# Filler products in TensorE's planned gaps, and score maxima taken four heads at a time, in a four-layer convolution and attention kernel

## The chip, the cores and the metric

The kernel runs on one core of a Trainium2 chip. The metric is device microseconds of one execution, from the first instruction to the last with what lies around them; lower is better. Seven executions before the change took 10873.29 to 10902.44 us, with a median of 10892.89 us.

Five engines work side by side, each through its own list of instructions in order: TensorE (PE, with its weight loads shown apart as PEld), VectorE (DVE), ScalarE (ACT), GpSimd (POOL) and SyncE (SP), which issues the transfers. TensorE writes its products to PSUM, which has eight banks of 128 x 512 fp32 here, and the others read them from there.

## What is computed

Four layers follow one another on x of shape (8, 256, 32, 32), eight samples of 256 channels and 1024 positions:

```python
# layer 0: attention with 4 heads (key 32, value 64), a 3x3 depthwise term, then a gated feed-forward and 8x8 FFTs
attn = softmax(einsum('bhkn,bhkm->bhnm', q, k) * SCALE)
out = einsum('bhdm,bhnm->bhdn', v, attn)
...
x = gelu(x1) * x2
...
# layer 1: group norm, attention with 8 heads of 32, a small MLP
attn = softmax(einsum('bhdi,bhdj->bhij', q, k) * temp)
...
# layer 2: quantised 1x1, 3x3, 1x1 convolutions, with integer codes
# layer 3: a Mamba block over four directions of the image (selective scan with 16 states)
x = _L0_conv_ref(x, ...); x = _L1_conv_ref(x, ...); x = _L2_conv_ref(x, ...); x = _L3_conv_ref(x, ...)
```

Softmax needs, for each of the 1024 rows of each head, the maximum over 1024 scores and the sum of exponentials. The change touches layers 0 to 2 only.

## The kernel before

**Two phases.** `phase_a` (line 258) does layers 0, 1 and 2 for all eight samples, `phase_b` (line 1059) layer 3. Each has a planner of its own. Nothing of `phase_b` is changed.

**The planner.** Work is written as Python generators ("strands") that yield one operation, or a list of operations on one engine with a cost, or a condition to wait for. `_Order.run` (line 231) keeps a planned clock for each engine. Again and again it takes, of all strands that are not waiting for a condition, the one whose operation could start first by the plan (ties by rank), emits it, and moves the engine's planned end (`free[e]`, line 253). The planned start is `_Order.start` (line 218): the latest of the engine's planned end, the planned ends of what the operation reads and overwrites, and 0.35 us (`LATENCY`) more where another engine did that. The order of instructions on each engine is thereby fixed when the program is built, and the scheduler of the framework adds the waits on the chip but moves nothing (`manual_schedule`, line 1041). All instructions are emitted by one helper, so the profile puts all of them on line 132 and groups are told apart by their tiles.

**Rooms.** A `_Room` (line 152) is a set of equal buffers. `left` lists those not taken, in the order in which they were put back; `take` takes the first. A buffer is put back when the plan *emits* its last reader, with the planned end of that reader, plus 0.35 us, kept in `last[tag, k]`; the next tile in that buffer has this as its `base`, before which nothing may write it. `bank` (line 287) is the room of the eight PSUM banks.

**Who uses banks.** The strand of a sample (`sample`, line 1020; layers at 653, 754, 865 and 956) takes single banks by `side()` for its projections. `maxima` (line 513) computes, for each head, each 128 rows (`t`) and each half of the keys (`j`), one bank of scores; VectorE takes the negated maximum of each row, ScalarE the exponentials with their sum. `MAXIMA` = 2 strands `some()` (line 520) share the list `todo` of (t, j, h) with h = 0 or 2, and take two heads at a time. Each head's product has 32 rows of the array (keys of 32 channels), and head h + e uses rows 32(h + e) to 32(h + e) + 31. `exponentials` (line 574) makes the attention itself: one bank for the output and, in each step, four banks of scores (cost `SCORES` = 1.3: four products of 32 rows, then four of 3 rows that subtract the maxima by means of the bf16 constant `minus`, -1.0 in 128 x 128, line 313), four exponentials on ScalarE, and four value products (`values`). Only one call of `exponentials` runs at a time: it fills `attending` while it runs. There are three calls of 16 steps for each sample, 24 in all.

**The limit on lent banks.** `may(n)` (line 395) is true when n banks are left and, while a call of `exponentials` is running, no more than `OTHERS` = 3 banks are then lent to everything else. So a set of four can't be lent while a call runs.

## Time and profile before

| | |
|---|---|
| median of 7 executions | 10892.89 us |
| the profiled execution | 10899.64 us |
| its span, first to last instruction | 10897.8 us |
| mean granted TensorE clock | 0.927 |
| TensorE busy | 9825.0 us (90%) |
| VectorE busy | 8475.8 us (78%) |
| ScalarE busy | 8686.1 us (80%) |
| GpSimd busy | 6713.9 us (62%) |
| maxima on VectorE (TENSOR_REDUCE of stats) | 1536, 979.9 us |
| last attention step of `phase_a` ends at | 3741 us |

The span runs from 0 to 10897.8 us on the profile's clock. `phase_a` fills about the first third; the numbers of the 40 slices show the seam as a jump in GpSimd's share and in the transferred bytes after the fourteenth slice. "Granted clock" is the share of TensorE's full clock that the hardware let through; in this execution it is always either 0.5 or 1. A busy share of TensorE counts a slowed product with its whole, longer duration. A product of fp32 operands shows as two matrix multiplications in the profile, one of bf16 operands as one.

### The profile page before, as it was taken

What the parts mean: (1) busy time and instruction counts of PE and PEld (TensorE: products, weight loads), DVE (VectorE), ACT (ScalarE), POOL (GpSimd) and SP (SyncE); (2) the same over time, 40 slices, a digit from 0 to 9 for tenths busy, and PEclk for the clock granted to TensorE, in tenths of its full rate; (3) what the DMA queues carried; (4) which work ended last, traced back from release to release, by engine and by line L of the source; (5) the groups of instructions that cost most, each with busy time, mean ns of one, the idle gap of its engine ahead of it and who ended that gap; (6) DMA issues with size and microseconds to landing.
All of it is one profiled execution on the core that took longest, in us unless ns stands there. A gap on an engine that the chain in (4) does not pass through costs nothing. (4 is left out here: it accounts for less than half of the span.)

```text
span 10897.8 us, 154085 instructions
## 1 busy us (share of the span) xinstructions
PE 9825.0 (90%) x56992; PEld 6320.2 (58%) x57104; DVE 8475.8 (78%) x9005; ACT 8686.1 (80%) x16270; POOL 6713.9 (62%) x3732
## 2 busy tenths in 40 slices
PE   8788998989999889999999999999989999999998
PEld 3233433333333257777777777777777777777776
DVE  4666556664735559898988998999889899898897
ACT  7666776777767568888989888888888888888887
POOL 2323012122221158888888888888888888888887
PEclk7778988888798789999999999999999999999999
DMA  1000000000000011111111111111111111111111
GB/s 38 5 4 5 2 9 6 8 2 9 5 3 1 12 38 48 47 47 52 50 41 56 44 46 54 45 48 53 45 49 48 50 48 46 51 50 42 55 42 46
DMA packets 210549, 367.85 MB, mean 34 GB/s; under 512 B 24241, under 2 KB 68657, under 8 KB 208770
## 3 DMA queue, kind: packets, MB, share of 16 engines
q1 hardware_dynamic: 209794, 358.00, 11.2%
q8 instruction: 448, 7.34, 0.3%
q14 instruction: 307, 2.51, 0.1%
HBM read 333.26 MB, written 14.16 MB: 32 GB/s over the span
## 5 line engine op out<-in xcount | busy, mean ns | idle before, releaser
L132 POOL TENSOR_TENSOR h<-h,cb 128x1024 f32<-128x1024 f32 x2048 | 4876.7, 2396 | 903.0 <-ACT st L132 440.5
L132 ACT ACTIVATE da<-dt,am 128x512 f32<-128x512 f32 x4096 | 2870.2, 713 | 512.4 <-DVE h L132 504.0
L132 DVE TENSOR_TENSOR_SCAN h<-da,st,db 128x512 f32<-128x512 f32 x2048 | 2468.6, 1259 | 177.4 <-PE db L132 96.1
L132 DVE TENSOR_TENSOR_SCAN h<-da,db 128x512 f32<-128x512 f32 x2048 | 2345.4, 1198 | 236.9 <-PE db L132 155.2
L132 ACT ACTIVATE dbu<-du,bT 128x512 f32<-128x512 f32 x3584 | 2474.9, 709 | 36.3 <-PE db L132 34.0
L132 PE MATMUL db<-ident,dbu 128*128 128x128 f32 x14336 | 2218.7, 280 | 177.2 <-DVE h L132 148.3
L132 PE MATMUL py<-ident,h 128*128 128x128 f32 x16384 | 2122.8, 275 | 91.9 <-POOL h L132 84.6
L132 PEld LDWEIGHTS db<-ident,dbu 128*128 128x128 f32 x14336 | 1671.4, 143 | 709.2 <-DVE h L132 375.2
L132 PEld LDWEIGHTS py<-ident,h 128*128 128x128 f32 x16384 | 1843.5, 141 | 169.0 <-POOL h L132 138.1
L132 DVE TENSOR_REDUCE stats<-bank 128x1 f32<-128x512 f32 x1536 | 979.9, 682 | 612.5 <-PE bank L132 610.7
L132 ACT ACTIVATE bank<-bank,stats 128x512 f32<-128x512 f32 x1536 | 1032.6, 691 | 393.8 <-DVE stats L132 387.9
L132 PE MATMUL bank<-big,big 32*128 32x512 f32 x4096 | 1075.7, 748 | 51.7 <-ACT bank L132 34.1
L132 POOL TENSOR_TENSOR mid<-mid,mid 128x961 f32<-128x961 f32 (+2 forms) x192 | 400.8, 2095 | 1064.6 <-ACT mid L132 700.8
L132 ACT ACTIVATE exps<-bank 128x512 f32<-128x512 f32 x1536 | 796.7, 619 | 259.2 <-PE bank L132 258.6
L132 PE MATMUL pp<-xi,cvd 128*128 128x512 f32 x2048 | 947.6, 606 | 9.6 <-ACT xs L132 3.4
L132 PE MATMUL db<-dg,du 128*128 128x128 f32 x4096 | 811.0, 280 | 0.0
L132 PEld LDWEIGHTS bank<-big,big 32*128 32x128 f32 x4096 | 427.7, 213 | 590.7 <-ACT bank L132 272.5
L132 POOL TENSOR_TENSOR dt<-dt,tmp 128x512 f32<-128x512 f32 x512 | 653.2, 1276 | 168.6 <-DVE tmp L132 146.5
L132 DVE TENSOR_TENSOR tmp<-dt,xs 128x512 f32<-128x512 f32 x256 | 603.4, 2357 | 191.9 <-POOL dt L132 191.7
L132 PEld LDWEIGHTS db<-dg,du 128*128 128x128 f32 x4096 | 638.0, 197 | 0.0
L132 PEld LDWEIGHTS pp<-xi,cvd 128*128 128x128 f32 x2048 | 378.1, 195 | 402.9 <-issue 387.9
L132 PE MATMUL bank<-big 32*128 32x512 f32 x2048 | 527.9, 740 | 53.0 <-ACT bank L132 43.5
(184 smaller groups left out, 11062.8 us busy)
## 6 DMA issues: line engine op xcount, KB each, us to landing
cb<-c_d SPq DMA_DIRECT2D x1024, 256.0 KB, 3.2
wi<-w_in SPq DMA_DIRECT2D x192, 192.0 KB, 3.5
cdb<-codes SPq DMA_DIRECT2D x48, 256.0 KB, 4.1
big<-in_x_dram SPq DMA_DIRECT2D x8, 1024.0 KB, 5.3
big<-big SPq DMA_DIRECT2D x16, 512.0 KB, 6.3
out_dram<-z SPq DMA_DIRECT2D x32, 256.0 KB, 2.5
low<-low SPq DMA_DIRECT2D x16, 128.0 KB, 2.4
codes<-cd SPq DMA_DIRECT2D x16, 128.0 KB, 1.7
```

What stands on the lines that cost most here:

```text
L132: return getattr(getattr(nc, self.engine), self.method)(*self.args, **self.kw)
```

## The change

Three things are added. First, the planner may be given a function `fill`, which it calls before it emits an operation on TensorE, with the planned start. Second, `phase_a` gives it one: it works out how long TensorE has been idle by the plan, counted from the time at which some bank (or the operation's own bank, where that is about to be overwritten) is free by the plan, and emits one product of the constant `minus` with itself (128 x 128 weights, 512 columns, bf16) for each 0.3 us (`FILL`) of it, into that bank, whose content nobody reads. Where it is a bank from the room, the one longest free by the plan is taken, and goes to the end of the list of `left`. The planner's clock isn't moved by these products. Third, `some()` in `maxima` waits until two banks may be lent, and then takes four heads at once where four may be lent and the next entry is h = 0 (it then takes the entry for h = 2 off the list too), two heads otherwise; the four products are one operation with a cost of 1.0 against 0.9.

```diff
@@ class _Order, __init__ and run
+        self.fill = None
...
             t, s = min(((self.start(s[2][1]), s) for s in ready), key=lambda x: (x[0], x[1][0]))
             cost, ops = s[2]
             e = ops[0].engine
+            if self.fill and e == "tensor":
+                self.fill(t, ops)
@@ phase_a, maxima
+    FILL = 0.3
...
             while todo:
+                yield lambda: not todo or may(2)
+                if not todo:
+                    break
+                n = 4 if may(4) and not todo[0][2] else 2
                 t, j, h = todo.pop(0)
-                bb = yield from two()
+                if n == 4 and todo:
+                    todo.pop(0)
+                bb = yield from some_banks(n)
                 ops = []
-                for e in range(2):
+                for e in range(n):
...
-                yield (0.9, ops)
-                for e in range(2):
+                yield (0.9 if n == 2 else 1.0, ops)
+                for e in range(n):
@@ phase_a, before the samples
+    def fill(gap, ops):
+        free, o = order.free.get("tensor", 0.0), ops[0]
+        spare = min(bank.left, key=lambda k: order.last.get((bank.tag, k), 0.0), default=None)
+        own = o.method == "matmul" and o.kw["start"] and o.args[0].shape[-1] == HALF and o.kw["rhs"].shape[0] > 3
+        since = min(
+            [order.last.get((bank.tag, k), 0.0) for k in bank.left] + [order.base.get(o.args[0].name, 0.0)] * own,
+            default=1e9,
+        )
+        n = int((gap - max(free, since)) / FILL)
+        if n < 1:
+            return
+        if spare is not None and order.last.get((bank.tag, spare), 0.0) <= since:
+            bank.left.remove(spare)
+            bank.left.insert(0, spare)
+            t = bank.take()
+        else:
+            t = None
+        out = o.args[0] if t is None else t
+        rhs = minus.unsqueeze(1).to_broadcast([P, 4, P])
+        for _ in range(n):
+            nc.tensor.matmul(out, lhsT=minus[:, : out.shape[0]], rhs=rhs, start=True, stop=True)
+        if t is not None:
+            bank.put(t)
+
+    order.fill = fill
```

## The prediction

> **What bounds the kernel now.** The profile's slices come first: they show where TensorE's clock is held down.

> ```profile
> PE   8788998989999889999999999999989999999998
> PEclk7778988888798789999999999999999999999999
> POOL 2323012122221158888888888888888888888887
> ```

> From the fifteenth slice on (layer 3) the clock is full nine tenths or more; the change doesn't touch that part. In layers 0 to 2 it is 0.7 to 0.9 although TensorE is busy 8 or 9 tenths. The table of stretches over 0 to 3741 us gives a mean of 0.84; as the clock is always 0.5 or 1, 32% of that time is at half clock.

> Next I split layers 0 to 2 by the 24 calls of `exponentials`, each from its first to its last exponential (64 apiece). The calls hold 1584 us, what lies between them 1916, the time before the first 199. Same view, columns as in the first line:

> ```profile
> core 0: us, PE busy (x) PEld busy (x) DVE busy (x) ACT busy (x) POOL busy (x), PEclk, DMA share, GB/s
> 3465.00:3529.00 64.00, 64.00 (x374) 19.93 (x374) 12.20 (x25) 46.16 (x98) 3.03 (x4) 1.00 0.00 1
> 2734.00:2977.00 243.00, 225.52 (x584) 92.38 (x583) 194.65 (x294) 177.75 (x434) 56.80 (x30) 0.77 0.02 6
> 3587.00:3666.00 79.00, 76.60 (x220) 28.90 (x218) 49.17 (x93) 46.65 (x128) 0.00 (x0) 0.50 0.00 1
> ```

> The first is a call: TensorE busy throughout at full clock, nothing else near it. Over the 24 calls TensorE is busy 1556 of 1584 us, clock 0.94. The second lies between calls: clock 0.77, with TensorE, VectorE and ScalarE all loaded. Over all stretches between calls the sums are TensorE 1612, VectorE 1531 and ScalarE 1291 of 1916 us, clock 0.76, so half clock for 2 x (1 - 0.76) = 48% of them. Counting the starts of the maxima's reductions, about 1300 of 1536 fall there or before the first call: calls and maxima take turns.

> What others wait for between calls, from the waits of that second stretch:

> ```profile
> DVE stats L132 <- PE bank L132: 31.1, 18, 4.1
> ```

> The same count over all stretches between calls: 377 us of VectorE's idle time end with a bank from TensorE, and no other cause passes 20. So the calls are bound by TensorE's work, and the rest is a chain in which TensorE, at half clock half of the time, is what VectorE waits for.

> **Why the clock falls.** The third row above is the key: 79 us with TensorE 97% busy, and half clock throughout. The products in it:

> ```profile
> 1518.58 1.93 PE L132 MATMUL bank<-big,w_m 128*64 128x512 f32 x4
> 1520.44 1.13 PE L132 MATMUL bank<-big,big 32*128 32x512 f32 x4
> 1521.50 1.93 PE L132 MATMUL bank<-big,w_m 128*64 128x512 f32 x4
> ...
> 3621.62 1.06 PE L132 MATMUL bank<-mid,codes_w 128*64 128x512 bf16 x2
> 3622.61 3.55 PE L132 MATMUL bank<-big,big 32*128 32x512 f32 x8
> ...
> 3712.64 1.14 PE L132 MATMUL bank<-big,big 32*128 32x512 f32 x8
> 3713.61 0.40 PE L132 MATMUL bank<-low,minus 3*128 3x512 bf16 x4
> 3713.93 1.07 PE L132 MATMUL bank<-exps,big 128*32 128x512 f32 x8
> 3714.93 1.14 PE L132 MATMUL bank<-big,big 32*128 32x512 f32 x8
> ```

> At full clock four passes of 128 rows take 1.86 us start to start, so one takes about 0.43 with the change of shape around it; a pair of heads (four passes of 32 rows) takes 1.06, eight passes of four heads 0.97. So 32-row products of different rows run together, and a pair fills half of the array. At half clock two pairs take 3.55 us. I cut the first 3.8 ms into windows of 3.41 us (all clock stretches but the last are multiples of it) and gave each window its array activity: streaming time of each product (0.427 us for 512 columns of an fp32 pass at full clock, half for bf16, double at half clock) times its share of rows and of columns, over the window. Of 70 half-clock windows with an activity of 0.75 or more, 64 are followed by full clock, of 300 below it 8. Of 54 full-clock windows below 0.3 all are followed by half clock, of 32 from 0.3 to 0.4 18, of 648 above it one. Between, the clock stays as it is. Pairs alone at half clock give about 0.45 (the most crowded bin: 60 windows, two left it). Hence the trap: once slow, a stage of pairs stays slow, however busy.

> [...]

> **The filler products.** One is 128 x 128, bf16, 512 columns: products of that form in layer 3 start 0.216 us apart at full clock (median of 705), 0.427 at half. They fill the whole array: in a window at half clock one adds 0.125 to the activity, so two or three lift a mixed window at 0.45 to 0.75, where it has idle time. At full clock 0.35 of a window is enough to stay up.

> Gain between calls: VectorE's 377 us of waiting for banks is the upper bound. A second way gives the same size: 48% of 1916 us is 914 us at half clock, TensorE about 0.79 busy there, and half of those 720 us, 360, is what half clock costs. The lower bound is nothing: VectorE is already busy 80% there, and its own operations may fill what is freed. I take half: **-190**. Gain in calls: clock 0.94 means 12% or 190 us at half clock, TensorE 98% busy, half of it lost: at most 93, I take **-80**, as calls begin at the clock that they find. Before the first call ScalarE is the fullest engine (153 us of 199): **-10**.

> Cost in calls: TensorE has no idle time there, so whatever the plan puts into a call lengthens it. The plan gives a step 1.3 + 0.9 = 2.2 us of TensorE; the four rows at 3712.64 show 2.29 in fact. By the code the next scores need four banks, three of which are free where nothing is lent and the fourth after the first exponential: 1.3 + 0.35 + 0.485 + 0.35 = 2.5, so 0.3 us of planned idle time, one product or none; with side work queued the plan has less. Bounds: nothing, and two products with two changes of shape in each of 384 steps: 384 x (2 x 0.216 + 2 x 0.2) = 319 us. A change of shape is 1.06 - 2 x 0.427 = 0.2 us. I take half a product and half a change: 384 x (0.108 + 0.1) = **+80**, since a value product and the scores after it differ in shape anyway.

> [...]

> Between calls the fillers are hidden by idle time of TensorE, which half the slow time would open: 1612 - 360 leaves 664 us idle of 1916. Without that cover each costs 0.216. A filler also waits for its bank's last reader, and it sends the longest-free bank to the end of the list, so that the next taker gets a later one.

> **Four heads at a time.** Never within calls (`may`). Two pairs alone cost 2 x 1.06, four heads 0.97 to 1.07: about 1.05 us saved, but nothing where two strands' pairs already stand side by side, as runs of eight passes at 1.07 show. I count 164 pairs between other products, so some 82 sets: 86 us of TensorE, of which a third matters where it is no longer the fullest engine: **-27**. All 650 pairs would be 325 x 1.05 = 341, nothing the other bound. Against it: four banks leave later, by two more evictions on ScalarE (0.691 us, with 0.233 for the sum partly hidden, near 0.78 each), so projections queued behind them wait. With some 20 such takes between calls for each sample, 8 x 20 x 1.56 = 250 us is the bound; most find another bank: **+30**.

> **Sum.** -190 - 80 - 10 + 80 - 27 + 30 = -197 against the profiled execution's 10899.64: 10703, called **10700**. That execution lies 7 us above the median of the seven; the span is 2 us shorter than its time.

> **Rivals.**
> *Fillers in the calls (slower).* The calls become longer than the rest becomes shorter. For: 98% busy there, so no slack. Against: the plan has little idle time in a full call. It decides where the fillers of a step cost more than what the other terms gain: (190 + 80 + 10 + 27 - 30) / 384 = 0.72 us. Three products with two changes of shape, 384 x 1.05 = 403, give 10900 - 277 + 403 = 11026; two products 10900 - 277 + 319 = 10942.
> *All of VectorE's waiting goes.* For: TensorE is its only large releaser. Against: VectorE is 0.99 busy in some slow stretches (1003 to 1075 us). -377 - 80 + 40 = -417: 10480.
> *The clock doesn't turn,* because the plan's idle time lies elsewhere than the real one, and the change doesn't do what it says: no gain, some fillers on the path, 10900 to 10950. Against: 0.125 a product against a step from 0.45 to 0.75.

> **How the numbers follow.** Forecast 0.55 (own range 10560 to 10860), all waiting gone 0.15, clock doesn't turn 0.08, calls longer 0.22. The range 10470 to 10990 leaves out part of the last (0.12) and of the second (0.06). 0.2% is 22 us, about what a measurement of this kernel can tell from no change. Faster by more: 0.55 + 0.15 = 0.70; within: 0.07, most of the third; slower: 0.23.

> **What would show it.** Clock of layers 0 to 2 from 0.84 to 0.93 or more; the stretches between calls together near 1700 us, the calls near 1584; VectorE's wait for banks about halved; runs of eight 32-row passes in the maxima; some 500 to 1500 products of `minus` with `minus`; layer 3 still 7157 us (10898 - 3741). I'm wrong if the calls grow by more than 250 us, or if the clock rises and the stretches between calls keep their length: then VectorE held them.

## The result, and the profile after

The changed kernel takes 10882.21 us (median of 26 executions), the kernel before 10882.99 us (63 executions beside it): ratio 1.0000, 95% interval 0.9995 to 1.0005. That is no change that can be measured; 10700 was forecast. The profiled execution of the changed kernel has a span of 10874.7 us.

The page of the changed kernel, first its slices, then two of its costlier groups (busy time and mean ns of one, then the idle time of the engine before them and what ended it):

```profile
PE   8899999999999889999999999999999999999998
...
PEclk8889899989899889999999999999999999999999
```

```profile
L132 DVE TENSOR_REDUCE stats<-bank 128x1 f32<-128x512 f32 x1536 | 979.0, 682 | 445.9 <-PE bank L132 444.5
...
L1050 PE MATMUL bank<-minus 128*128 128x512 bf16 (+1 forms) x2087 | 595.9, 418 | 66.9 <-ACT bank L132 50.1
```

The change does what it says. 2087 fillers are in the trace (line 1050), the granted clock is a tenth higher in 11 of the first 14 slices, and VectorE waits 446 us ahead of its maxima, against 613 us before. (This fall is not what it seems: the sets of four alone have it too, 453 us in e1 below, and the fillers alone don't, 610 us in e2.) The windows of the changed kernel, first all of layers 0 to 2, then the counterpart of the 243 us between two calls that the prediction showed:

```profile
core 0: us, PE busy (x) PEld busy (x) DVE busy (x) ACT busy (x) POOL busy (x), PEclk, DMA share, GB/s
0.00:3741.00 3741.00, 3530.91 (x15921) 1275.89 (x15922) 2147.98 (x3213) 2628.21 (x5703) 845.08 (x439) 0.92 0.03 7
2703.32:2951.39 248.07, 226.61 (x737) 83.56 (x735) 201.17 (x313) 181.16 (x448) 54.23 (x29) 0.88 0.01 2
```

The clock of layers 0 to 2 rises from 0.84 to 0.92: by the records of the clock, half clock falls from 1229 us to 567. In the second row it rises from 0.77 to 0.88, and the stretch lasts 248 us instead of 243. VectorE's wait for banks, which was to fall by half, is still 30.2 us there (31.1 before):

```profile
DVE stats L132 <- PE bank L132: 30.2, 23, 5.8
```

Split as in the prediction, from the profiles (the stretches between calls are here all 23 of them, short ones included, 1960 us before; the prediction counted 1916 in the longer ones):

| us, with mean clock | before | after |
|---|---|---|
| before the first call | 199, 0.70 | 198, 0.81 |
| 24 calls | 1583, 0.94 | 1497, 0.99 |
| 23 stretches between calls | 1960, 0.77 | 2037, 0.89 |
| end of the last call | 3741 | 3732 |
| from there to the end | 7157 | 7143 |

The calls became 86 us shorter and the rest 77 us longer. That is partly a move: 124 maxima on VectorE start inside calls, 233 before. Two things are therefore mixed, and the first experiments separate them.

### The profile page after: what moved, and what is told of

Read it like the earlier page. It is cut to its first block, busy times and chain, and to the rows that moved or that the text cites. A ratio compares the mean times of both kernels' runs of the same rounds, so it can differ in the third digit from the quotient of the medians.

```text
span 10874.7 us, 158299 instructions
## 1 busy us (share of the span) xinstructions
PE 9990.8 (92%) x59079; PEld 6280.0 (58%) x59191; DVE 8439.4 (78%) x9005; ACT 8696.0 (80%) x16270; POOL 6708.9 (62%) x3732
## 5 line engine op out<-in xcount | busy, mean ns | idle before, releaser
L132 POOL TENSOR_TENSOR h<-h,cb 128x1024 f32<-128x1024 f32 x2048 | 4877.6, 2397 | 890.7 <-ACT st L132 436.9
L132 ACT ACTIVATE da<-dt,am 128x512 f32<-128x512 f32 x4096 | 2869.9, 713 | 508.8 <-DVE h L132 500.6
L132 DVE TENSOR_TENSOR_SCAN h<-da,st,db 128x512 f32<-128x512 f32 x2048 | 2467.8, 1258 | 173.7 <-PE db L132 96.9
L132 DVE TENSOR_TENSOR_SCAN h<-da,db 128x512 f32<-128x512 f32 x2048 | 2345.0, 1198 | 222.8 <-PE db L132 146.3
L132 ACT ACTIVATE dbu<-du,bT 128x512 f32<-128x512 f32 x3584 | 2474.6, 709 | 33.7 <-PE db L132 31.5
L132 PE MATMUL db<-ident,dbu 128*128 128x128 f32 x14336 | 2215.3, 280 | 173.1 <-DVE h L132 142.9
L132 PE MATMUL py<-ident,h 128*128 128x128 f32 x16384 | 2119.2, 275 | 94.2 <-POOL h L132 86.9
L132 PEld LDWEIGHTS db<-ident,dbu 128*128 128x128 f32 x14336 | 1668.3, 143 | 705.1 <-DVE h L132 371.9
L132 PEld LDWEIGHTS py<-ident,h 128*128 128x128 f32 x16384 | 1839.8, 141 | 173.2 <-POOL h L132 141.7
L132 ACT ACTIVATE bank<-bank,stats 128x512 f32<-128x512 f32 x1536 | 1021.6, 669 | 393.0 <-DVE stats L132 383.6
L132 DVE TENSOR_REDUCE stats<-bank 128x1 f32<-128x512 f32 x1536 | 979.0, 682 | 445.9 <-PE bank L132 444.5
L132 POOL TENSOR_TENSOR mid<-mid,mid 128x992 f32<-128x992 f32 (+2 forms) x192 | 400.4, 2093 | 1129.5 <-ACT mid L132 663.7
L132 ACT ACTIVATE exps<-bank 128x512 f32<-128x512 f32 x1536 | 797.4, 618 | 256.4 <-PE bank L132 255.9
L132 PE MATMUL pp<-xi,cvd 128*128 128x512 f32 x2048 | 947.2, 606 | 9.6 <-ACT xs L132 3.4
L132 PE MATMUL bank<-big,big 32*128 32x512 f32 x4096 | 917.3, 679 | 19.3 <-ACT bank L132 16.5
L132 PE MATMUL db<-dg,du 128*128 128x128 f32 x4096 | 809.2, 280 | 0.0
L132 POOL TENSOR_TENSOR dt<-dt,tmp 128x512 f32<-128x512 f32 x512 | 652.9, 1275 | 175.2 <-DVE tmp L132 153.1
L132 DVE TENSOR_TENSOR tmp<-dt,xs 128x512 f32<-128x512 f32 x256 | 606.1, 2367 | 188.8 <-POOL dt L132 188.6
L1050 PE MATMUL bank<-minus 128*128 128x512 bf16 (+1 forms) x2087 | 595.9, 418 | 66.9 <-ACT bank L132 50.1
L132 PEld LDWEIGHTS db<-dg,du 128*128 128x128 f32 x4096 | 636.2, 196 | 0.0
L132 PEld LDWEIGHTS pp<-xi,cvd 128*128 128x128 f32 x2048 | 378.1, 195 | 402.3 <-issue 387.6
L132 PEld LDWEIGHTS bank<-big,big 32*128 32x128 f32 x4096 | 291.9, 194 | 464.3 <-issue 275.4
```

The source lines that it names most:

```text
L132: return getattr(getattr(nc, self.engine), self.method)(*self.args, **self.kw)
L1050: nc.tensor.matmul(out, lhsT=minus[:, : out.shape[0]], rhs=rhs, start=True, stop=True)
```

## The experiments

Every ratio is to the kernel before on the same chip. "Between" is the sum of the 23 stretches between calls, "calls" that of the 24 calls, each with its mean clock, "end" the end of the last call, all from one profile; before has 1960 at 0.77, 1583 at 0.94 and 3741. What follows that end is the same layer 3 in all kernels, and it takes 7131 to 7169 us in the profiles, so differences of some 20 us between single profiles prove nothing.

| run | us | ratio (95% interval) | between | calls | end |
|---|---|---|---|---|---|
| e1 sets of four only | 10905.76 | 1.0022 (1.0013 to 1.0030) | 2057, 0.75 | 1499, 0.96 | 3753 |
| e2 fillers only | 10866.40 | 0.9983 (0.9974 to 0.9992) | 1962, 0.87 | 1554, 0.99 | 3721 |
| e3 corner fillers | 11049.43 | 1.0149 (1.0133 to 1.0165) | 2064, 0.80 | 1614, 0.94 | 3889 |
| e4 double fillers | 11089.12 | 1.0190 (1.0176 to 1.0204) | 2083, 0.95 | 1633, 1.00 | 3913 |
| e5 fillers where the plan is idle | 10882.82 | 1.0000 (0.9991 to 1.0009) | 1959, 0.85 | 1556, 0.98 | 3721 |
| e6 fillers outside calls | 10871.00 | 0.9985 (0.9976 to 0.9994) | 1954, 0.87 | 1566, 0.95 | 3725 |
| e7 sets with six banks free | 10887.48 | 1.0003 (0.9994 to 1.0012) | 2034, 0.75 | 1504, 0.95 | 3735 |
| e8 short products, fillers | 10731.28 | 0.9862 (0.9847 to 0.9877) | 1869, 0.81 | 1515, 0.98 | 3575 |
| e9 short exponentials, fillers | 10819.82 | 0.9941 (0.9925 to 0.9958) | 1931, 0.88 | 1548, 0.99 | 3678 |
| e10 short maxima, fillers | 10770.03 | 0.9898 (0.9883 to 0.9913) | 1869, 0.90 | 1542, 0.99 | 3617 |
| e11 half-length fillers | 10899.05 | 1.0012 (1.0003 to 1.0020) | 1985, 0.81 | 1555, 0.98 | 3743 |
| e12 after, six banks free | 10861.57 | 0.9978 (0.9969 to 0.9987) | 2031, 0.88 | 1490, 0.99 | 3719 |
| e13 short products, no fillers | 10750.40 | 0.9878 (0.9865 to 0.9892) | 1869, 0.73 | 1546, 0.93 | 3606 |
| e14 short maxima, no fillers | 10788.45 | 0.9920 (0.9904 to 0.9935) | 1861, 0.79 | 1567, 0.94 | 3627 |
| e15 runs of three or more | 10851.07 | 0.9969 (0.9958 to 0.9980) | 1967, 0.85 | 1543, 0.98 | 3707 |
| e16 e12, runs of three or more | 10873.99 | 0.9997 (0.9988 to 1.0005) | 2050, 0.85 | 1482, 0.98 | 3729 |
| e17 short products, corner fillers | 10870.80 | 0.9987 (0.9977 to 0.9996) | 1952, 0.74 | 1574, 0.93 | 3719 |
| e18 runs of six or more | 10831.18 | 0.9950 (0.9938 to 0.9963) | 1959, 0.83 | 1541, 0.97 | 3696 |

**The two halves of the change.** e1 has the sets of four and no fillers. e2 has the fillers and the pairs of before; the free-bank list is put back as it was after each filler, so that every other instruction stands in the order of before.

```diff
@@ e1, against after
-    order.fill = fill
+    order.fill = None
@@ e2, against before: fill as in after, but
+            was = list(bank.left)
             bank.left.remove(spare)
...
             bank.put(t)
+            bank.left[:] = was
```

> The sets of four heads stay, no filler is emitted. Theory G (the gain of the clock is given back: the fillers lift the clock of layers 0 to 2 from 0.84 to 0.92, and take as much TensorE time as the clock saves): within 25 us of before, clock of layers 0 to 2 near 0.84, since sets of four save TensorE time only where it isn't the limit. Theory F (the sets of four lose what the fillers gain): 40 to 150 us slower than before. Theory E (TensorE's clock isn't what holds layers 0 to 2; other engines and the order of the list do): within 25 us.

> Pairs as before and 1833 fillers; all other instructions stand in the order of before on every engine, and the list of free banks is put back after each filler. Theory G: within 25 us of before, clock of layers 0 to 2 about 0.9. Theory F: 40 to 150 us faster. Theory E: within 25 us.

The sets alone cost 23 us, the fillers alone gain 16. In e1 the calls lose 84 us and the rest gains 96 without a filler in the kernel: the move of maxima out of the calls belongs to the sets. With e2 the question stands bare. The windows of before and of e2 for the stretches over 3.5 us between calls (sums, then means of one stretch):

```profile
sum 1941.60, PE 1637.98 PEld 672.29 DVE 1544.20 ACT 1306.41 POOL 555.64; mean PE 96.35 PEld 39.55 DVE 90.84 ACT 76.85 POOL 32.68
```

```profile
sum 1940.33, PE 1772.39 PEld 679.94 DVE 1541.66 ACT 1305.11 POOL 555.78; mean PE 110.77 PEld 42.50 DVE 96.35 ACT 81.57 POOL 34.74
```

The clock goes from 0.77 to 0.87 over all stretches, and they last as long as before to 2 us. TensorE is busy 134 us more, the others the same. Over layers 0 to 2, counting each product from its start to the next less the idle time before that, the kernel's own products fall from 3362 to 3029 us, the fillers take 478 and idle time falls from 356 to 212: -333 + 478 - 144 is nothing.

**What a filler costs without its effect.** e3 has e2's fillers in e2's places, but on a corner of the array: 64 x 64 instead of 128 x 128, same columns. That is a quarter of the array, and by the prediction's measure a quarter of the activity, for the same time on TensorE (by the clock it counts for more, as the last section shows). e4 has more than twice as many (`FILL` 0.15).

```diff
@@ e3, against e2
-        rhs = minus.unsqueeze(1).to_broadcast([P, 4, P])
+        rhs = minus[:HM].unsqueeze(1).to_broadcast([HM, 4, P])
...
-            nc.tensor.matmul(out, lhsT=minus[:, : out.shape[0]], rhs=rhs, start=True, stop=True)
+            nc.tensor.matmul(out[: min(HM, out.shape[0])], lhsT=minus[:HM, : min(HM, out.shape[0])], rhs=rhs, start=True, stop=True)
@@ e4, against e2
-    FILL = 0.3
+    FILL = 0.15
```

> As e2, but each filler uses 64 x 64 of the array, so it streams as long at full clock (512 columns, bf16) with a quarter of the activity. Theory G: the clock stays near 0.84 and the fillers' time is paid without the gain, 100 to 300 us slower than before. Theory E: within 25 us of before, as the fillers lie in idle time of TensorE. Theory F says nothing of it.

> As e2 with one filler for each 0.15 us of planned idle time: 4140 in place of 1833, 2307 x 0.216 = 498 us more of TensorE at full clock. Theory G: the clock near 0.95 and 100 to 400 us slower than before, as the clock has less left to give than the fillers take. Theory E: within 50 us of before, unless TensorE becomes the limit.

e3 is 1.5% slower, its last call ends 148 us later than before's. The same windows of e3, between calls and then the calls themselves:

```profile
sum 2049.24, PE 1920.26 PEld 722.71 DVE 1565.70 ACT 1312.16 POOL 566.38; mean PE 106.68 PEld 40.15 DVE 86.98 ACT 72.90 POOL 31.47
...
sum 1614.11, PE 1599.84 PEld 530.61 DVE 487.69 ACT 1151.66 POOL 213.25; mean PE 66.66 PEld 22.11 DVE 20.32 ACT 47.99 POOL 8.89
```

So the fillers aren't free. All 23 stretches together are 104 us longer than before's, the calls 31. The reason isn't that a corner filler is dearer in itself. In the traces of e2 and e3 both kinds start 0.216 us apart at full clock and 0.427 at half, and at full clock a 32-row fp32 product starts 0.309 us after a whole filler ahead of it and 0.306 after a corner one. Only beside a 128 x 128 product does the corner take some 0.09 us more (0.306 against 0.216), which some 100 such places between calls make 9 of the 104 us. Against e3, e2 shows what full activity brings: 102 us between calls, 60 in the calls. Between calls cost and gain are equal. e4 overshoots: clock 0.95 between calls, and both parts longer than before, by 123 and 50 us.

**Fewer or shorter fillers.** e5 puts in only as many as raise the plan's activity over 3.4 us to half, by the fillers and the products themselves; e6 leaves them out while a call runs; e11 halves their columns.

```diff
@@ e5, against e2 (a list `lately` holds the planned activity of the last WINDOW)
+    WINDOW, TARGET = 3.4, 0.5
...
+        more = max(0, math.ceil((TARGET * WINDOW - now) / 0.216))
+        filler(gap, ops, min(n, more))
@@ e6, against e2
-        if n < 1:
+        if n < 1 or attending:
@@ e11, against e2
-        rhs = minus.unsqueeze(1).to_broadcast([P, 4, P])
+        rhs = minus.unsqueeze(1).to_broadcast([P, 2, P])
...
-            nc.tensor.matmul(out, lhsT=minus[:, : out.shape[0]], rhs=rhs, start=True, stop=True)
+            nc.tensor.matmul(out[:, : HALF // 2], lhsT=minus[:, : out.shape[0]], rhs=rhs, start=True, stop=True)
```

> As e2 (order of before, pairs), but the fillers are counted out: the planner keeps the array activity of the last 3.4 us of the plan (each product's streaming time at full clock times its share of rows and columns, fillers included) and adds only as many as lift it to 0.5: 1109 in place of 1833. Theory G (each filler costs TensorE time on the path, e3 against before: 167 us / 1833 = 0.09 us each; the clock gives 183 us back, e3 against e2): the clock stays near e2's and the cost falls to 1109 x 0.09 = 101 us, so some 80 us faster than before. Theory H (the fillers that are left out were the free ones, or the clock falls with their number): within 25 us of e2, that is 0 to 40 us faster than before.

> As e2, with no filler while a call of exponentials runs by the plan: 1273 in place of 1833. In e2 the calls took 1554 us, with corner fillers 1614, before 1583. If the calls owe their clock to the stretch before them (my prediction's term for calls), they come to about 1525 and the whole is some 45 us faster than before. If their own fillers keep the clock up, the calls come to 1583 again and the whole is within 20 us of before.

> As e2, in the same order, with as many fillers (1833) of 256 columns in place of 512: 1833 x 0.108 = 198 us of TensorE less, and half of their activity. Theory G, with the cost going by time (about 0.08 us for a filler of 0.216): the cost falls by some 75 us; the clock falls to about 0.945 over the whole and gives 30 to 50 back: 25 to 45 us faster than e2, 40 to 60 faster than before. If a filler costs by being there (a change of shape, a wait for its bank): the cost stays and the clock falls, 0 to 30 us slower than before.

None beats e2. In e5 some 1060 fillers up to the last call's end instead of 1740 leave the stretches where they were (1959) at a clock of 0.85. In e6 the calls lose their own fillers, and their clock falls back to 0.95; they still take 17 us less than before, probably since the stretch ahead of them leaves them at a better clock (0.87 in the stretches, 0.77 before). e11 is the worst of the three: its stretches are 23 us longer than e2's at a clock of 0.81. Half the length gave up more clock than it saved time. At this point the runs could also be read as if the clock between calls didn't matter at all and the fillers cost nothing there (theory E; theory G has a cost and a gain that cancel), since 0.77, 0.85 and 0.87 gave the same length; e3 was the only run against it.

**Which engine holds the stretches.** In e8 to e10 one engine's share of the maxima is made shorter, on e2: bf16 products of `minus` in place of the fp32 products of q and k (same 32 rows), exponentials over half a bank, or maxima over half a bank. e13 and e14 are e8 and e10 without fillers.

```diff
@@ e8, against e2
-                    ops.append(
-                        T.matmul(bb[e], lhsT=q[r, t * P : (t + 1) * P], rhs=k[r, hs(j)], start=True, stop=True)
-                    )
+                    op = T.matmul(bb[e], lhsT=q[r, t * P : (t + 1) * P], rhs=k[r, hs(j)], start=True, stop=True)
+                    op.kw = dict(op.kw, lhsT=minus[r, :], rhs=minus[r].unsqueeze(1).to_broadcast([32, 4, P]))
+                    ops.append(op)
@@ e9, against e2
+                    op.args = (bb[e][:, : HALF // 2], bb[e][:, : HALF // 2], AF.Exp)
@@ e10, against e2
+                    op.args = (m, bb[e][:, : HALF // 2], AX.X, ALU.max)
@@ e13 against e8, e14 against e10
-    order.fill = fill
+    order.fill = None
```

> As e2, in the same order, but each product of the maxima multiplies the bf16 constant with itself (32 rows, 512 columns, one pass) in place of q and k in fp32: the maxima are not those of the scores. A pair takes about 0.27 us more than nothing in place of 1.06, 768 x 0.8 = 600 us of TensorE less. Theory G (TensorE's time in the stretches between calls sets their length, and the fillers take there what the clock gives): the stretches, 1962 us in e2, fall by 200 us or more. Theory E (something else holds them at about 1960 as long as TensorE keeps up; it did before at half clock, and with corner fillers it no longer did): they fall by less than 60 us.

> As e2, in the same order, but ScalarE's exponential of each bank of the maxima covers 256 of the 512 columns: half of each row's sum is left out. 1536 x about 0.21 us = 330 us of ScalarE less. Theory G: the stretches between calls keep their 1962 us within 40. Theory E, where ScalarE's part of the chain (product, maximum, exponential, next product in that bank) holds them: 100 to 300 us less. Where it is VectorE alone that holds them: less than 40 us.

> As e2, in the same order, but VectorE's maximum of each bank covers 256 of the 512 columns: the other half of the scores doesn't count for the maximum. 1536 x about 0.27 us = 410 us of VectorE less. Theory G: the stretches keep their 1962 us within 40. Theory E, where VectorE's work or its part of the chain holds them: 100 to 350 us less; where it is ScalarE alone: less than 40.

> As e8 (products of the maxima replaced by short products of the constant), in the same order, without any filler. In e8 TensorE stands idle 436 us before the last call's end, so fillers have cover there. Theory G (the clock is worth its time wherever the fillers have cover): without them the clock falls below 0.93 over the whole and the time is 40 to 120 us above e8's 10731. Theory E (TensorE's clock doesn't set the time as long as TensorE has slack): within 25 us of e8. If fillers cost even under cover: 30 or more us below e8.

> As e10 (VectorE's maximum over half of each bank, the other half of the scores left out), in the same order, without any filler. Shortening the maxima gave 96 us from e2 to e10 with fillers. Theory G (without fillers the half clock of TensorE is what binds between calls): less than 60 us against before. Theory E (the chain through VectorE binds with and without them): 75 to 115 us against before, that is about e10's time.

The page of e10 shows the shortened group:

```profile
L132 DVE TENSOR_REDUCE stats<-bank 128x1 f32<-128x256 f32 x1536 | 580.6, 417 | 828.7 <-PE bank L132 825.8
```

VectorE has 399 us less work (979.9 to 580.6), waits 829 us for banks instead of 610, and the kernel is 96 us faster than e2. ScalarE with 330 us less gives 47, TensorE with 472 us less (32-row products 1396 to 924 us) gives 135; as the clock is lower there (0.81 between calls against e2's 0.87), its whole busy time up to the last call's end falls by 370 us only. Each engine's work counts by a seventh to more than a quarter: none of the three is the bound by itself. The wait for a bank is a handover in a chain that goes round through all three and through eight banks, and what one of them saves comes back mostly as its own idle time.

With and without fillers the stretches of the lightened kernels are alike: 1869 and 1869 us (e8, e13), 1869 and 1861 (e10, e14). That spoke once more for a clock of no importance between calls, so the corner fillers were tried there too.

```diff
@@ e17, against e8
-        rhs = minus.unsqueeze(1).to_broadcast([P, 4, P])
+        rhs = minus[:HM].unsqueeze(1).to_broadcast([HM, 4, P])
...
-            nc.tensor.matmul(out, lhsT=minus[:, : out.shape[0]], rhs=rhs, start=True, stop=True)
+            nc.tensor.matmul(out[: min(HM, out.shape[0])], lhsT=minus[:HM, : min(HM, out.shape[0])], rhs=rhs, start=True, stop=True)
```

> As e8 (short products of the constant for the maxima), with the 1833 fillers on a 64 x 64 corner of the array, as in e3: the fillers' time without their clock, in a kernel whose TensorE stands idle 654 us without fillers (e13). The stretches between calls were 1869 us in e13 (no fillers, clock 0.73 there) and 1869 in e8 (full fillers, clock 0.81). Theory E (neither the clock nor the fillers set their length as long as TensorE has slack): 1869 again within 15, whole time 10740 to 10770. Theory G (both act, and cancelled in e8 as in e2): about 0.06 us for each of 1200 fillers, 1925 to 1970, whole time 10805 to 10860.

The windows between calls of e13 (no fillers), e17 (corner fillers) and e8 (whole ones), in this order:

```profile
sum 1848.40, PE 1288.06 PEld 442.67 DVE 1539.96 ACT 1300.02 POOL 558.20; mean PE 80.50 PEld 27.67 DVE 96.25 ACT 81.25 POOL 34.89
```

```profile
sum 1933.78, PE 1629.30 PEld 571.60 DVE 1559.74 ACT 1300.57 POOL 567.09; mean PE 95.84 PEld 33.62 DVE 91.75 ACT 76.50 POOL 33.36
```

```profile
sum 1847.71, PE 1496.42 PEld 524.28 DVE 1543.03 ACT 1298.45 POOL 559.47; mean PE 93.53 PEld 32.77 DVE 96.44 ACT 81.15 POOL 34.97
```

This settles it for G. In e13 TensorE is busy only 1288 of 1848 us. Corner fillers add 341 us of busy time to it and, over all stretches, 83 us of length (1869 to 1952) at almost the same clock (0.73 and 0.74). Whole fillers raise the clock to 0.81 and take the 83 us off again. Equal lengths with and without fillers are a cost and a gain of the same size, here as in e2, and not two zeros. One limit: a corner filler may itself run longer than a whole one, as it leaves the clock low (576 us for the traced fillers of e3, 478 for those of e2), so part of what the table calls the clock's gain is the fillers' own shortening. The sums hold; the split is that between e3 and e2.

Where a filler stands in the way can be seen in places. The timeline of the changed kernel before the first call, at half clock:

```profile
153.91 3.59 PE L1050 MATMUL bank<-minus 128*128 128x512 bf16 x8
157.44 1.99 PE L132 MATMUL bank<-big 32*128 32x512 f32 x12
...
158.60 0.69 DVE L132 TENSOR_REDUCE stats<-bank 128x1 f32<-128x512 f32 x1 [2.70 <-PE bank L132]
```

Eight fillers of 0.43 us run for 3.59 us where the plan saw a gap; a pair for the maxima comes behind them, and VectorE has waited 2.70 us when the first maximum starts. How much of this the pair would have had to wait anyway isn't in these lines.

**The banks.** e7 is e1 with sets of four only where six banks are free instead of four, so that two stay behind; e12 is the changed kernel with the same edit.

```diff
@@ e7 against e1, e12 against after
-                n = 4 if may(4) and not todo[0][2] else 2
+                n = 4 if may(6) and not todo[0][2] else 2
```

> As e1 (sets of four, no fillers), but a set is taken only where six banks may be lent, so that two stay for projections. e1 was 23 us slower than before. Theory B (sets starve the other strands of banks): within 10 us of before. Theory O (the sets move maxima out of the calls and side work with them, whatever the banks): 15 to 30 us slower again.

> The changed kernel, with sets of four only where six banks may be lent (29 sets in place of 90, by the planner's count). e1 and e7 put the sets at +23 us with four free and 0 with six free, both without fillers; the fillers alone (e2) at -18. If the two parts add up: about 16 us faster than before, against 1 for the changed kernel. If they don't (the fillers make the sets worth their banks): no faster than the changed kernel.

The loss goes: e1's 23 us become 0.3 in e7, and e12 is 24 us faster than before where the changed kernel stands at 1 us. By the plan there are 90 sets in the changed kernel and 29 with six banks free. This is what theory B expected, and theory O didn't: in e7, too, few maxima start inside calls (136; 123 in e1, 233 before), without the loss. But e7 has a third of the sets, and a cost of each set whatever the banks, a third of 23 us, would lie within e7's interval. So that the loss lies in the banks fits and isn't shown. No run shows that the sets gain time: e12 stands at 0.9978, the fillers alone at 0.9983.

**Long gaps only.** e15 and e18 are e2 with fillers only where the gap takes at least three or six of them; e16 is e12 with at least three.

```diff
@@ e15 against e2, e16 against e12 (e18 against e2 has 6)
-        if n < 1:
+        if n < 3:
```

> As e2, with fillers only where the plan leaves room for three or more: 1509 fillers in 196 places in place of 1833 in 435. e11 halved the fillers' length and lost 30 us against e2. If the cost lies in the many short places (each a change of shape and a delay where the chip has no idle time): 20 to 50 us faster than e2, clock near 0.95. If the cost goes by the fillers' time, as in e4: about 324 x 0.08 = 26 us faster, less what the clock loses, so 0 to 20 us faster than e2. If neither and the chain through the other engines sets the time: within 10 us of e2.

> As e12 (the changed kernel with sets of four only where six banks may be lent, 24 us faster than before), with fillers only where the plan leaves room for three or more. If e15's restriction gains, it gains here as much; 25 to 60 us faster than before if it does, 15 to 30 us if it doesn't.

> As e15 (34 us faster than before), with fillers only where the plan leaves room for six or more: 1017 fillers in 73 places in place of 1509 in 196. If the places cost and few long ones keep the clock up: 10 to 30 us faster than e15. If the calls lose the clock that the places inside them gave (the calls of e15 took 1543 us, of e2 1554, before 1583): 10 to 30 us slower than e15.

By the traces e2 has 1833 fillers in 443 places, e15 1509 in 204, e18 1017 in 73, and they gain 16, 29 and 53 us. e18 is the fastest version found, and faster than both kernels. Its windows, between calls and in the calls:

```profile
sum 1938.36, PE 1757.79 PEld 720.63 DVE 1543.79 ACT 1303.75 POOL 555.22; mean PE 109.86 PEld 45.04 DVE 96.49 ACT 81.48 POOL 34.70
...
sum 1540.98, PE 1520.55 PEld 549.28 DVE 513.57 ACT 1146.22 POOL 226.60; mean PE 63.36 PEld 22.89 DVE 21.40 ACT 47.76 POOL 9.44
```

Between calls it is at 1959 us, as before. Its gain by the profile is in the calls: 1541 against 1583 us, at a clock of 0.97 with 53 traced fillers in them; e2 has 424 there and 1554. What remains of its lead over e2 in the medians (35 us; 25 at the end of the last call) may lie partly in the scatter of single profiles. That the number of places is what costs isn't shown: e15 and e18 speak for it, but e16, with the same edit as e15, is slower than e12. e18 with the sets at six free banks wasn't tried.

## Why the prediction was wrong

**What was right.** That the low clock went with a low activity of the array, and that fillers lift it: 0.84 to 0.92 in layers 0 to 2, 0.77 to 0.89 between calls. In the changed kernel 58 of 59 half-clock windows with an activity of 0.75 or more are followed by full clock, and none of 112 below; none of 855 full-clock windows above 0.4 falls. The calls didn't grow, and layer 3 stayed. One of the two conditions under which the prediction called itself wrong came true: "the clock rises and the stretches between calls keep their length" (in e2 to 2 us; in the changed kernel they even grew by 77). What it would conclude from that, "then VectorE held them", the runs don't show: with 399 us less work for VectorE (e10 against e2) the stretches lost only 93.

**The step that failed** is "Between calls the fillers are hidden by idle time of TensorE, which half the slow time would open". They cost 104 us there (e3 against before), 83 where TensorE has far more idle time (e17 against e13). With some 1200 traced fillers that is 0.07 to 0.09 us for each, a third to two fifths of the 0.216 that the prediction named as the price without cover (a fifth to a quarter of the 0.34 and 0.37 us that they took in these two runs, often at half clock), and it was put at nothing. In e13 TensorE was idle 654 us in layers 0 to 2, and fillers still cost. The reading that fits, argued from the waits and not shown by itself: idle time in a round chain ends with a release by another engine, at a moment that the plan doesn't hit, and a filler that runs just then holds back the product behind it in the queue, with every engine that waits for that product.

**The gain between calls** (-190, half of VectorE's waiting) was measured as -102 and -83, near a quarter of the 377. The prediction took VectorE's wait as TensorE's doing; e8 to e10 show that the three engines share the round, so that 472 us less of TensorE's products gave 135. That this is the whole reason for the size isn't shown.

**The other terms.** Gain in calls: -80 forecast, -60 measured (e2 against e3). Cost in calls: +80 forecast, +31 measured (e3 against before), +28 in e17 against e13. Both had the right sign, and their sum, -29, is about all that the fillers bring. Before the first call: -10 forecast; the profiles give +6 in e2 and -1 in the changed kernel, which is nothing. Sets of four: -27 + 30 forecast; a cost is there, and probably in the banks, as the prediction said, but no gain shows against it: +23 alone, and 0 with two banks kept back. The number of sets was near (82 forecast, 90). The change of shape was read as 0.2 us; at full clock in e2 a filler starts 0.520 us after the last 32-row fp32 product ahead of it, where 0.429 would do (128 x 128 fp32 passes start that far apart at full clock in both kernels), and the next one starts 0.309 after the filler, where 0.216 would do, so that 0.2 is the way in and the way out together. The bound of 319 us for the calls charges it for each way; by these numbers it is about 237.

With the measured values the sum is -102 + 104 - 60 + 31 + 0 + 23 = -4, against -1 measured. This says that the two halves of the change add up, and no more: the first four terms, taken by way of e3, are by construction e2 less before.

**The rivals.** "All of VectorE's waiting goes" and "fillers in the calls" fall: between calls VectorE's wait for banks is 413 us after and 399 before, over all stretches, and the calls are not longer. "The clock doesn't turn" came nearest in size, for the wrong reason: the clock turned. The case that came was not among them: the clock turns, the calls gain a little, and between calls a filler costs what its clock returns.

## What to carry to other kernels

A filler in an in-order queue is not free because its engine has idle time (here each cost 0.07 to 0.09 us between calls, also where TensorE was idle 654 us without fillers): price it by a run in which it takes the same time and has no effect, and subtract. Where several engines hand a small set of buffers round, a saving on any one of them counts by a fraction, which a run with that engine's work made shorter shows (here a seventh to somewhat over a quarter), so half of a wait is too much to expect. Fewer fillers, in the longest gaps only, can bring more than many (here 1017 against 1833). A larger set of buffers taken at once lost time here, and lost none where two more had to be free first, which also made the sets fewer.

## What the runs showed of the hardware

Busy time as the measure doesn't fit e3: its fillers kept TensorE busy for 1920 of 2049 us between calls (94%), e2's for 1772 of 1940 (91%), and its clock was 0.80 there against 0.87.
